# Two transformer blocks with routed experts: a third buffer for routed rows, 28 scatters a sequence, and k's transposes one step sooner

## The chip, the cores and the metric

The kernel runs on one core of a Trainium2 chip. The metric is the device time of one execution in microseconds; three runs of the kernel before are shown, and one further execution was profiled. The core has TensorE (PE, with its weight loads shown as PEld), VectorE (DVE), ScalarE (ACT), GpSimd (POOL) and SyncE (SP). SP issues most DMAs; POOL issues those whose row addresses are computed at run time.

## The reference

Eight sequences of 512 tokens with 256 features go through two blocks. All arithmetic is float32.

```python
x = x + attention0(layernorm(x))   # 16 query heads, 4 key/value heads of 16, rotary, causal
x = x + ffn0(layernorm(x))         # 32 experts, 8 per token, inner 96, weights renormalized over the 8
x = x + attention1(layernorm(x))   # 16 heads of 16, biases, scores masked with -10000
x = x + ffn1(layernorm(x))         # 16 experts, 2 per token, inner 176, and 2 shared experts
```

An expert computes `silu(x @ wg) * (x @ wu) @ wd`, and the token's routing weight scales its result.

## The kernel before

**Stages.** Attention 0 runs over the eight sequences, then all experts of block 0, then attention 1 over the sequences, then all experts of block 1. Tokens are sent to experts through DRAM: each token's normalized row, with its routing weights behind it (288 floats, 1152 bytes), is scattered into the slab of each of its 8 experts (`xg`, L470), one scatter for 128 tokens and one of the 8 choices. A sequence so has 4 x 8 = 32 scatters of 144 KB. The expert stage loads tiles of 128 rows from the slabs (L1339), multiplies them, and writes the results to `yg`.

**Attention 0** is written as a plan for TensorE. Each round treats one sequence in ten steps. A step begins with the scores of some heads (L745), then ScalarE's exp over 2048 columns (L750), then the letters of that step's word in `PLAN0`: "c" a product with the values (L768), "t" the transposes of its result (`ot`, L780, freed by VectorE's product L784), "m" the causal masks (L756), and one step of a chain for "p" and "q" (the next sequences' load, projection, rotary and transposes, `before`, L997), "a" and "o" (the last sequences' output projection, layernorm and routing, `finish`). "q" becomes "p" and "a" becomes "o" in the next round. What is left of a chain at the end of a round is drained there, in the order p, o. The scores have a single PSUM buffer of four banks (`st`), and all small products share three banks in turn (`bank`).

`before` has ten steps: two for loading, one for the statistics, four for the tokens' projections, two for the transposes of q (L1053), and one for k: four transposes (L1059) and two scaled copies on ScalarE (L1062, L1063). For sequence 1 two more steps come first. Three of them run as "q" in one round. In the next round six run as "p", so that k's step is the one that the drain does. At the end of the round in which sequence 3's chain is drained, the tables for the experts' tiles are made as well (`tables`; products `ex` L1238 and `ro` L1240).

**Routed rows.** `layernorm_steps` writes the normalized rows (`xn_f`, L361) to a tile of the pool `xn_rows`, which has two buffers; `route` adds the weights and puts the 32 scatters on the list `waiting`, in step 1 of the round two after that of their sequence. `send` takes scatters off the list: at each step of attention 0 as many as `SENT[0]` says, each paced by (that is, made to wait for) the step's exp. So 32 leave in a round. A buffer is written again only after its scatters have landed. The last sequence is routed in the expert stage.

**The expert stage** of block 0 is a pipeline over pairs of tiles: `load` in step s, the transposes of the rows in step s+4 (L1353), gate and up in s+5 (L1385), the transposes of h in s+6 (L1404), down in s+7 (L1414, copied out by L1419). There are 53 pairs in a first part, which holds only rows of sequences 0 to 3, and 86 in a second, which waits for every scatter. The down weights (`dw`, L1536) are asked for in step 3 of the program; SP issued three of their six DMAs ahead of the first row loads. From step 7 on, two waiting scatters are sent in each step, paced by that step's copy (`beside.made`).

The lines that set the order and its numbers:

```python
PLAN0 = "ocmoo otom poaaom mc taapma comapa tpm qqqm cmpp taaam"
SENT = ((3, 3, 4, 3, 3), (1, 1, 1, 1, 1))      # by step modulo 5; first entry: attention 0
send(SENT[att.n][at % len(STEPS)], None if att.n else att.newest)
if s >= stages[-1][1]:                          # expert stage, step 7 and later
    send(2, beside.made)
```

Of the kernel before, what the change touches and what calls it, by code (L numbers as in the profile page):

```python
# [8 lines left out]
F32 = mybir.dt.float32  # L9
# [8 lines left out]
P = 128  # L18
NB, T, D = 8, 512, 256
NT = T // P  # L20
ND = D // P
H, HKV, DH = 16, 4, 16
NG = 4
# [5 lines left out]
N1 = N1R + IS1  # L29
C0 = N0 // P  # L30
C1 = -(-N1 // P)
PLAN0 = "ocmoo otom poaaom mc taapma comapa tpm qqqm cmpp taaam"
TAIL0 = "otoaoaoaoa"
PLAN1 = "cooggm ootggm oaggm coaggm toapggm acoggpm taaopggm ppaoggm caopggm taopppm"
TAIL1 = "otaaoaaaoaoaoaa"
PB = (3, 2)
SENT = ((3, 3, 4, 3, 3), (1, 1, 1, 1, 1))
SPLIT = (4, 6)
AHEAD = 3
FIRST = 18  # L40
# [60 lines left out]
def two_blocks_kernel(  # L101
# [14 lines left out]
    nc = tc.nc  # L116
# [167 lines left out]
    kept = {}  # L284
# [23 lines left out]
    def inverse_root(var, lnp, name):  # L308

        v = lnp.tile([P, NT], F32, tag="v", name=f"v_{name}")  # L310
        nc.vector.tensor_scalar(v, var, LN_EPS, None, ALU.add)
        bits = lnp.tile([P, NT], I32, tag="bits", name=f"bits_{name}")
        nc.vector.tensor_scalar(bits, v.bitcast(I32), 1, None, ALU.arith_shift_right)
        r = lnp.tile([P, NT], F32, tag="rstd", name=f"rstd_{name}")
        nc.vector.tensor_scalar(r.bitcast(I32), bits, -1.0, float(0x5F3759DF), ALU.mult, ALU.add)
        w = lnp.tile([P, NT], F32, tag="w", name=f"w_{name}")
        for _ in range(3):
            nc.vector.scalar_tensor_tensor(w, r, -0.5, r, ALU.mult, ALU.mult)
            nc.vector.tensor_tensor(w, w, v, ALU.mult)
            nc.vector.scalar_tensor_tensor(r, w, 1.5, r, ALU.add, ALU.mult)  # L320
        return r
# [13 lines left out]
    lasting, turned0, roots, sums = [], [], {}, {}  # L335

    def layernorm_steps(x, lnp, name, tag="xn", bufs=1, spare=0, behind=lambda: None):


        def later():  # L340
            return tc.issue_after(behind()) if behind() else ExitStack()

        stats = lnp.tile([P, NT, 6], F32, tag="stats", name=f"stats_{name}")
        mv = lnp.tile([P, NT, 2], F32, tag="mv", name=f"mv_{name}")
        for t in range(NT):
            with later():
                nc.vector.bn_stats(out=stats[:, t, :], in_=x[:, t, :])
            nc.vector.bn_aggr(out=mv[:, t, :], in_=stats[:, t, :])
            if t % 2:
                yield  # L350
        with later():
            rstd = inverse_root(mv[:, :, 1], lnp, name)
        roots[name] = rstd
        yield
        if tag is None:
            return rstd
        kept = lasting and tag == "xn_rows"
        xn = (lasting[0] if kept else lnp).tile([P, NT, D + spare], F32, tag=tag, name=f"xn_{name}", bufs=2 if kept else bufs)
        for t in range(NT):
            with later():  # L360
                nc.vector.tensor_scalar(  # L361
                    xn[:, t, :D], x[:, t, :], mv[:, t, 0:1], rstd[:, t : t + 1], ALU.subtract, ALU.mult
                )
            if t % 2:
                yield
        return xn
# [484 lines left out]
    def send(n, pace):  # L851
        for work, t, i in waiting[:n]:
            work(t, i, pace)
        del waiting[:n]

    def planned(att, before, after, plan, tail, ahead=None):
# [15 lines left out]
        for b in range(NB):  # L872
# [5 lines left out]
            for at, works in enumerate(plan.split()):  # L878
                att.scores(b, at)
                send(SENT[att.n][at % len(STEPS)], None if att.n else att.newest)  # L880
                drain(begun)
# [32 lines left out]
            )  # L914
        return wo

    def v_tiles(pool, n, heads, engine):

        tiles = []
        for i in range(n):  # L920
            v1 = pool.tile([P, NT, heads * (DH + 1) + 32 - DH - 1], F32, tag="v1", name=f"v1_{i}", bufs=n)
            engine.memset(v1, 1.0)
            tiles.append(v1)
        return tiles
# [4 lines left out]
    def fast0(awp, lnp, atp, late, ptp, ps, bank):  # L929
# [25 lines left out]
        kept = {0: ahead[0]}  # L955
# [6 lines left out]
        turn = []  # L962
        for which in ("cos", "sin"):
            lo, hi = A0[which]
            f = awp.tile([DH, T], F32, tag="turnf", name=f"{which}f", bufs=1)
            nc.scalar.dma_start(out=f, in_=a0[:DH, lo:hi])
            tr = bank(f"{which}t")[:, : NT * DH].rearrange("p (t d) -> p t d", t=NT)
            for t in range(NT):
                nc.tensor.transpose(tr[:, t, :], f[:, t * P : (t + 1) * P], ident[:DH, :DH])
            w = awp.tile([P, NT, DH], F32, tag=which, name=f"{which}0")  # L970
            nc.vector.tensor_copy(w, tr)
            turn.append(w)
        cos, sin = turn
        v1s = v_tiles(awp, 2, NG, nc.gpsimd)
        n_h = H + HKV
        hf = DH // 2

# [322 lines left out]
    def experts(n, gu, dn, mp, ps, again, beside, load_last):  # L1300

        name = f"m{n}{'g' * again}"
# [139 lines left out]
        with tc.manual_schedule(engines={ENG.PE}):  # L1442
            for s in range(len(jobs) + stages[-1][1]):
                for stage, lag in stages:
                    if 0 <= s - lag < len(jobs):
                        stage(*jobs[s - lag])
                if s == 3:
                    load_last()
                beside.step(s)
                if s >= stages[-1][1]:  # L1450
                    send(2, beside.made)
            beside.finish()

    def most_rows(b, again):
# [153 lines left out]
    def drain(part):  # L1608
        for _ in part:
            pass  # L1610
# [119 lines left out]
    with ExitStack() as s2:  # L1730
        lasting.append(s2.enter_context(tc.tile_pool(name="xn_rows", bufs=2, reuse_waits="tile")))
        PARTS = 4
        with ExitStack() as s:
            awp, lnp, atp, late, ptp, smp, ps = pools(s, 0, False)
            bank = banks(ps, 3)
            att, before = fast0(awp, lnp, atp, late, ptp, ps, bank)
            route, _ = ffn_parts(smp, bank)
            gw0 = gpool.tile([P, E0 * GU0], F32, tag="gu", name="gw0")

            def after0(b):  # L1740
                if b == NB - 1:
                    return
                kept = keep_x(b, x_after[0])
                yield from routed0(b, lnp, bank, route)
                if b < PARTS:
                    with tc.issue_after(kept):
                        load_gate_up(gw0, f0, I0, N0, b, PARTS)
                if b == 1:
                    yield from biases1(smp, bank)
                if b == SPLIT[0] - 1:  # L1750
                    yield from tables(lays[0], smp, bank, 0)


            with tc.manual_schedule(engines={ENG.PE}):
                planned(att, before, after0, PLAN0, TAIL0)


        with ExitStack() as s1:
            wp1 = s1.enter_context(tc.tile_pool(name="attn_w1", bufs=1, reuse_waits="tile"))
            gat = s1.enter_context(tc.tile_pool(name="gather", bufs=1, reuse_waits="tile"))  # L1760
            w1, loads1 = weights1(wp1)
            last = all_experts(0, gw0, gat, weights=loads1)
            with ExitStack() as s:
                awp, lnp, atp, late, ptp, smp, ps = pools(s, 1, False)
                v1s = v_tiles(awp, 2, H, nc.vector)
                bank = banks(ps, 3)
                att, before = fast1(w1, v1s, lnp, atp, late, ptp, ps, bank, last)
                route, shared = ffn_parts(smp, bank)
                gw1 = gpool.tile([P, E1 * GU1], F32, tag="gu", name="gw1")

                def ahead1(b):
                    if b >= AHEAD:
                        fetched = fetch_x(b, x_after[0], "a1")
                        with tc.issue_after(fetched):
                            load_gate_up(gw1, f1, I1, N1R, b - AHEAD, NB - AHEAD)
                        yield
                        yield from gathers(b)

                def after1(b):
                    name = f"f1_{b}"  # L1780
                    xn = layernorm(xs[b], lnp, name, "xn_rows", 2, 2 * E1)
                    yield
                    xT = yield from turned(xn, lnp, bank, name)
                    yield from route(1, b, xn, xT, name, False)
                    yield from shared(w1["s"], xT, xs[b], name)
                    if b < NB - RING:
                        keep_x(b, x_after[1])
                    if b == SPLIT[1] - 1:
                        yield from tables(lays[1], smp, bank, 0)

                with tc.manual_schedule(engines={ENG.PE}):
                    planned(att, before, after1, PLAN1, TAIL1, ahead1)
                out_of = not_fine(bank)
        lasting.clear()
# [245 lines left out]
```

## Time and profile before

| | us |
|---|---|
| median of three runs | 1529.74 (1527.24 to 1532.12) |
| the profiled execution | 1526.4 |
| its span, first to last instruction | 1524.7 |
| first exp of attention 0 | 30.25 |
| first expert row loads issued by SP | 378.37 |
| first copy of an expert result (L1419) | 399.0 |
| TensorE busy | 1386.1 (91%) |
| VectorE busy | 949.7 (62%) |
| GpSimd busy | 812.7 (53%) |
| ScalarE busy | 654.7 (43%) |

Of GpSimd's 812.7 us, 326.7 are the 320 scatters of routed rows of both blocks (L470, 1021 ns each, with a gap of 0.30 us after each), and 402.5 are the 256 gathers of the first experts' results (L1494). The table comes from the first part of the page and from the engines' instructions in order of time. Durations in the text are of the one profiled execution. A row of waits reads: who waited, for whom, total us, how many times, the longest.

### The profile page before, as it was taken

The numbers are of one execution on the slowest core, as the hardware profiler recorded it, in microseconds if no ns is written. First come the engines' busy times: TensorE is split into PE (matmuls) and PEld (weight loads), VectorE is DVE, ScalarE is ACT, GpSimd is POOL, SyncE is SP. The second block draws the span as 40 slices with busy tenths as digits, with TensorE's granted clock in tenths as the row PEclk, the third lists the DMA queues.
The fourth block names the chain that finished last, engine by engine and source line by source line (L and its number), as shares of the span: only waits on it lengthen the run. The fifth ranks groups of instructions, "written<-read, shape, count | busy, mean of one in ns | idle before, by whom it ended". The sixth has DMA issues, their size and how long they took to land.

```text
span 1524.7 us, 29311 instructions
## 1 busy us (share of the span) xinstructions
PE 1386.1 (91%) x9608; PEld 951.1 (62%) x9608; DVE 949.7 (62%) x3141; ACT 654.7 (43%) x857; POOL 812.7 (53%) x674
## 2 busy tenths in 40 slices
PE   5788988887899999999997889999999988999994
PEld 3444544444789889999894445455465454777773
DVE  4668888876475557655565567677577564544454
ACT  2556666654233323333334546646646642122222
POOL 0004777777366100288878887788887204243342
PEclk8999999999899999999999999999999999999996
DMA  2023555435999786899998555665553015353346
GB/s 82 15 70 99 162 166 164 151 135 155 296 298 294 251 254 197 225 259 269 269 271 163 70 70 104 101 146 84 114 70 91 32 31 177 96 173 111 117 159 232
DMA packets 229311, 237.20 MB, mean 156 GB/s; under 512 B 77820, under 2 KB 209281, under 8 KB 229154
## 3 DMA queue, kind: packets, MB, share of 16 engines
q1 hardware_dynamic: 172930, 145.73, 32.4%
q0 software_dynamic: 55872, 89.18, 25.4%
q8 instruction: 83, 1.36, 0.4%
q14 instruction: 74, 0.61, 0.1%
q10 hardware_dynamic: 352, 0.33, 0.1%
HBM read 125.79 MB, written 110.92 MB: 155 GB/s over the span
## 4 chain that ended last, share of the span: by engine, by line
PE 58%; POOL 11%; issue 5%; DMA 4%; DVE 3%; ACT 3%; SPq 0%; DVEq 0%; ACTq 0%; POOLq 0%
PE gu_m L1385 18%; PE y_m L1414 12%; POOL x_a L1494 10%; PE xgT_m L1353 5%; PE st_a L745 4%; PE o_a L768 3%; PE hT_m L1404 3%; ACT p_a L750 2%; PE sg_f L503 2%; PE sy_f L516 2%; PE su_f L503 2%; PE y_a L842 1%; PE v_a L1129 1%; DMA xg<-xn_f,rows_f 1%; DMA xg_m<-xg 1%
## 5 line engine op out<-in xcount | busy, mean ns | idle before, releaser
L1494 POOL DMA_INDIRECT x_a<-yg,yrows x256 | 402.5, 1572 | 218.0 <-DMA xg_m<-xg 131.0
L470 POOL DMA_INDIRECT xg<-xn_f,rows_f x320 | 326.7, 1021 | 344.0 <-ACT sums L1023 131.1
L750 ACT ACTIVATE p_a<-st_a 128x2048 f32<-128x2048 f32 x160 | 300.4, 1877 | 187.0 <-PE st_a L745 85.3
L1385 PE MATMUL gu_m<-gw,xgTs_m 128*128 x1416 | 304.4, 359 | 1.2 <-DVE xgTs_m L1355 1.2
L1385 PEld LDWEIGHTS gu_m<-gw,xgTs_m 128*128 128x128 f32 x1416 | 236.3, 193 | 26.0 <-DVE xgTs_m L1355 1.7
L745 PE MATMUL st_a<-qT_a,kT_a 32*128 32x512 f32 (+3 forms) x2048 | 192.7, 480 | 58.8 <-ACT p_a L750 49.2
L1414 PE MATMUL y_m<-dw,hTs_m 96*128 (+1 forms) x860 | 215.8, 380 | 2.1 <-issue 2.1
L756 DVE TENSOR_TENSOR p_a<-p_a,causal 128x512 f32<-128x512 f32 x256 | 169.6, 687 | 74.1 <-ACT p_a L750 73.7
L1419 ACT COPY ys_m<-y_m 128x512 f32<-128x512 f32 x177 | 103.6, 585 | 170.0 <-PE y_m L1414 150.9
L745 PEld LDWEIGHTS st_a<-qT_a,kT_a 32*128 32x128 f32 x2048 | 92.2, 190 | 133.5 <-ACT p_a L750 72.8
L1355 DVE COPY xgTs_m<-xgT_m 128x512 f32<-128x512 f32 x177 | 121.5, 687 | 80.0 <-PE xgT_m L1353 75.7
L768 PE MATMUL o_a<-p_a,v 128*32 128x512 f32 (+3 forms) x2048 | 158.9, 450 | 3.6 <-DVE p_a L756 3.6
L1414 PEld LDWEIGHTS y_m<-dw,hTs_m 96*128 96x128 f32 (+1 forms) x860 | 149.7, 190 | 16.1 <-issue 2.3
L1377 DVE SCALAR_TENSOR_TENSOR h_m<-h_m,xg_m,gu_m 128x96 f32<-128x96 f32 (+1 forms) x354 | 104.2, 325 | 83.1 <-ACT h_m L1390 39.1
L1427 POOL DMA_INDIRECT yg<-ys_m,to_m x76 | 80.3, 1057 | 125.8 <-ACT ys_m L1419 113.1
L768 PEld LDWEIGHTS o_a<-p_a,v 128*32 128x32 f32 x2048 | 57.7, 112 | 122.0 <-issue 92.0
L1405 DVE COPY hTs_m<-hT_m 96x256 f32<-96x256 f32 (+1 forms) x177 | 84.0, 474 | 76.0 <-PE hT_m L1404 75.6
L1393 ACT ACTIVATE h_m<-gu_m 128x192 f32<-128x192 f32 x139 | 45.9, 330 | 181.2 <-PE gu_m L1385 162.1
L1353 PE MATMUL xgT_m<-ident,xg_m 128*128 128x128 f32 x708 | 110.3, 278 | 11.2 <-DMA xg_m<-xg 7.3
L1353 PEld LDWEIGHTS xgT_m<-ident,xg_m 128*128 128x128 f32 x708 | 88.4, 143 | 33.3 <-issue 9.4
L1404 PE MATMUL hT_m<-ident,h_m 128*96 128x128 f32 (+1 forms) x430 | 76.8, 274 | 0.0
L1404 PEld LDWEIGHTS hT_m<-ident,h_m 128*96 128x96 f32 (+1 forms) x430 | 52.8, 125 | 16.7 <-issue 6.4
(266 smaller groups left out, 1591.7 us busy)
## 6 DMA issues: line engine op xcount, KB each, us to landing
xg_m<-xg SPq DMA_DIRECT2D x354, 144.0 KB
yg<-ys_m SPq DMA_DIRECT2D x139, 256.0 KB
g<-yg SPq DMA_DIRECT2D x16, 512.0 KB
xg<-zeros SPq DMA_DIRECT2D x50, 144.0 KB
xg<-xn_f,rows_f POOLq DMA_INDIRECT x320
x_after<-x_in SPq DMA_DIRECT2D x8, 512.0 KB
x_a<-x_after SPq DMA_DIRECT2D x8, 512.0 KB
x_a<-yg,yrows POOLq DMA_INDIRECT x256
```

Source lines behind the costliest of these rows:

```text
L470: inst = nc.gpsimd.indirect_dma_start(out=lay.xg, out_offset=bass.IndirectOffsetOnAxis(ap=rows[:, t, i : i + 1], axis=0), in_=xn[:, t, :], ...
L745: nc.tensor.matmul(st[:, g, lo : lo + T - j * P], kT[r, j * P : (j + 1) * P], qT[r, j * P :], start=True, stop=True,)
L750: self.newest = nc.scalar.activation(pt, st, AF.Exp, scale=SCALE).ins
L756: self.masked = nc.vector.tensor_tensor(d, d, causal.unsqueeze(1).to_broadcast([P, NG, P]), ALU.mult).ins
L768: nc.tensor.matmul(o[32 * g : 32 * g + 32, j * P :], v1[:, j, v_at + g * (DH + 1) :][:, :32], pt[:, g, lo : lo + T - j * P], start=(step = ...
L1353: nc.tensor.transpose(tr[:, j, c, :], xg[:, j, c * P : (c + 1) * P], ident)
L1355: nc.vector.tensor_copy(xT, tr)
L1377: nc.vector.scalar_tensor_tensor(h[:, j, :], h[:, j, :], xg[:, j, D:][:, bass.ds(offs[part, i + j][2], 1)], gus[j][:, inner:], ALU.mult, A ...
L1385: nc.tensor.matmul(gus[j], xT[:, j, c, :], gu[:, bass.ds(at + c * 2 * inner, 2 * inner)], start=(c == 0), stop=(c == ND - 1),)
L1404: nc.tensor.transpose(hp[:n_in, q, j, :], h[:, j, lo : lo + n_in], ident)
L1414: nc.tensor.matmul(y[:, j, :], hT[:n_in, q, j, :], dn[:n_in, bass.ds(at + q * D, D)], start=(q == 0), stop=(q == n_ch - 1),)
L1494: inst = nc.gpsimd.indirect_dma_start(out=xs[b][:, t, :], out_offset=None, in_=lay.yg[: most_rows(b, again), :], in_offset=bass.IndirectOf ...
```

## The change

Five edits are made, and nothing of the arithmetic changes.

- `layernorm_steps` gives the rows of sequences 2 and 5 of block 0 a buffer of their own (tag `more_rows`), beside the two that the others share, so that a buffer comes round after three sequences instead of two.
- `SENT[0]` goes from 3, 3, 4, 3, 3 to 3, 3, 2, 3, 3: 28 scatters in a round of ten steps instead of 32.
- In the expert stage, steps 2 to 6 send two scatters each as well, paced by the step's row load (`beside.load`).
- `PLAN0` has a third "p" in step 8. For sequences 2 to 7 that is k's step of `before`; for sequence 1 it is the second of the four projections.
- Two changes of memory: in attention 1 the second tile of values is put into the `more_rows` buffer, and in the start of attention 0 the cos and sin tables are read through the buffer `kr` instead of one of their own.

```diff
-PLAN0 = "ocmoo otom poaaom mc taapma comapa tpm qqqm cmpp taaam"
+PLAN0 = "ocmoo otom poaaom mc taapma comapa tpm qqqm cmppp taaam"
-SENT = ((3, 3, 4, 3, 3), (1, 1, 1, 1, 1))
+SENT = ((3, 3, 2, 3, 3), (1, 1, 1, 1, 1))
...
-        xn = (lasting[0] if kept else lnp).tile([P, NT, D + spare], F32, tag=tag, name=f"xn_{name}", bufs=2 if kept else bufs)
+        if kept and name.startswith("f0_") and int(name[3:]) % 3 == 2:
+            tag, bufs = "more_rows", 1
+        elif kept:
+            bufs = 2
+        xn = (lasting[0] if kept else lnp).tile([P, NT, D + spare], F32, tag=tag, name=f"xn_{name}", bufs=bufs)
...
-    def v_tiles(pool, n, heads, engine):
+    def v_tiles(pools, heads, engine):
...
-        for i in range(n):
-            v1 = pool.tile([P, NT, heads * (DH + 1) + 32 - DH - 1], F32, tag="v1", name=f"v1_{i}", bufs=n)
+        for i, pool in enumerate(pools):
+            tag = "more_rows" if pool in lasting else "v1"
+            v1 = pool.tile([P, NT, heads * (DH + 1) + 32 - DH - 1], F32, tag=tag, name=f"v1_{i}", bufs=pools.count(pool))
...
-            f = awp.tile([DH, T], F32, tag="turnf", name=f"{which}f", bufs=1)
+            f = atp.tile([DH, T], F32, tag="kr", name=f"{which}f", bufs=1)
...
-        v1s = v_tiles(awp, 2, NG, nc.gpsimd)
+        v1s = v_tiles([awp, awp], NG, nc.gpsimd)
...
                 if s >= stages[-1][1]:
                     send(2, beside.made)
+                elif s > 1:
+                    send(2, beside.load)
...
-                v1s = v_tiles(awp, 2, H, nc.vector)
+                v1s = v_tiles([awp, lasting[0]], H, nc.vector)
```

## The prediction

> **What bounds the kernel now.** I read the page's slices first, then a table of windows cut at each sequence of the first attention, then the waits, then single engines in order of time. The change touches three places: the first attention (78 to 376 us of the span), the start of the first expert stage (376 to 404), and the tail of that stage's scatters (to 503). All work is serial across these stages, so a microsecond won or lost on TensorE's path in any of them is one in the total.
>
> The windows, cut at the first exp of each sequence (columns: length; busy time and instructions of PE, PEld, DVE, ACT, POOL; clock; DMA share; GB/s):
>
> ```profile
> 121.60:163.50 41.90, 36.29 (x344) 19.75 (x344) 34.48 (x135) 26.05 (x28) 24.04 (x23) 1.00 0.46 139
> ...
> 206.00:248.00 42.00, 36.12 (x344) 19.71 (x340) 34.44 (x135) 26.00 (x27) 32.24 (x33) 1.00 0.56 175
> 248.00:292.40 44.40, 38.62 (x354) 20.43 (x354) 37.65 (x156) 26.01 (x27) 34.65 (x33) 0.97 0.42 146
> 292.40:334.30 41.90, 37.13 (x336) 19.30 (x336) 30.33 (x115) 25.15 (x25) 32.76 (x31) 0.95 0.38 132
> ```
>
> A sequence takes 42 us whether POOL is busy 24 or 33 us in it; only that from 248 is 2.3 us longer. So the scatters, back to back on POOL from 150 to 384 us, hardly slow the attention. What they could slow is VectorE's write of normalized rows (L361), which waits for a buffer whose scatters have landed, and the waits say what that is worth in all:
>
> ```profile
>   DMA xg<-xn_f,rows_f: 0.7, 3
> ```
>
> Three waits, 0.24 us each. TensorE's own waits over the sequences are these:
>
> ```profile
> PE st_a L745 <- ACT kT_a L1062: 9.5, 7, 1.6
> ...
> PE ro L1240 <- DVE otok_a L784: 1.9, 1, 1.9
> ```
>
> **Third buffer: -0.5 us.** At most the 0.7 us above goes, and only where VectorE leads: the chain of waits runs through it after two of the three (272.7 and 356.5), 2 x 0.24 = 0.5. Rows of sequence s join the waiting list in step 1 of round s+2 and leave from step 2 on. Before, 26 go in that round and 6 in the next two steps, so none is left over. With 28 a round, sequences 0 to 3 finish at round 3 step 3, round 4 step 4, round 5 step 6 and round 6 step 7. The row that reuses their buffer is written about step 5 of rounds 4, 5, 6 and 7, eight steps later at least. No new wait. Without the third buffer, 28 would make one. The shared cos/sin buffer costs nothing: its readers come before the first key write, in TensorE's order already. Nor does attention 1's value tile in the third buffer: sequence 5's scatters, its last readers, land in the expert stage long before.
>
> **k's transposes, five ordinary boundaries: +0.6 us.** This is one boundary now, ScalarE then TensorE:
>
> ```profile
> 200.67 1.07 ACT L1054 COPY qT_a<-qT_a 128x512 f32<-128x512 f32 x2
> 202.21 1.88 ACT L750 ACTIVATE p_a<-st_a 128x2048 f32<-128x2048 f32 x1 [0.47 <-PE st_a L745]
> 203.98 0.68 ACT L1062 ACTIVATE kT_a<-kT_a,half 128x512 f32<-128x512 f32 x1
> 204.55 0.69 ACT L1063 ACTIVATE kT_a<-kT_a,half 128x512 f32<-128x512 f32 x1
> ```
>
> ```profile
> 201.00 1.15 PE L745 MATMUL st_a<-qT_a,kT_a 32*128 32x384 f32 x16
> 202.07 0.66 PE L780 MATMUL ot_a<-ident,osb_a 128*128 128x128 f32 x4
> 202.57 0.60 PE L1059 MATMUL kT_a<-ident,kr_a 128*128 128x128 f32 x4
> 204.72 1.14 PE L745 MATMUL st_a<-qT_a,kT_a 32*128 32x512 f32 x8 [1.55 <-ACT kT_a L1062]
> ```
>
> The wait of 1.55 us looks like the prize, but most of it stays: the scores buffer (one copy) is free only when the exp begun at 202.21 ends. Where nothing but an exp stands ahead, scores start 1.94 us after its start (209.29 to 211.23 in the next steps); here 2.51 (202.21 to 204.72). So the move, which issues no DMA, saves 0.57. It is paid for at once: the four transposes now stand before the 201.00 scores, which follow the q transposes without a gap, +0.55 on TensorE (0.60 less the overlap of the record). ScalarE must also make its two k copies (1.25 us together) after the q copies end at 201.74, so its exp comes near 202.9 instead of 202.21: +0.69. Net 0.12 a boundary. Ends: -0.5 if the exp is not delayed, +0.55 if ScalarE takes it before the k copies (then the wait stays and TensorE's 0.55 is added). I take 0.12, nearest to the order in which the inputs come ready: 5 x 0.12 = 0.6.
>
> **The sequence from 248 us: -2.0 us.** There the end of a round also drains the planner's tables. Products take one of three PSUM banks in turn. Before, the order is q, q, ot, k, ex, ro, so ro gets ot's bank, and ot is freed by a VectorE product that comes late (L784, 289.7): TensorE stands 1.9 us and the next scores follow at 290.23. With k ahead the order is q, q, k, ot, ex, ro: ro gets k's bank, freed by ScalarE some 2 us earlier. The round should fall from 44.4 to the 42 of its neighbours. I take 2.0 of 2.3, since VectorE's masks of the last step end at 291.8 and limit the product after the scores; ends 0 (another VectorE item holds TensorE) and -2.3. **A rule against a row** here: the Trainium skill, "TensorE: Matmul & The Clock Gate", "What's actually happening", has the clock halve after an idle window of about 3.4 us. By it a pause of 1.9 us costs 1.9. The trace shows half clock (0.50) at 290 to 292 after this pause, and the eight scores take 2.02 us against 1.14, some 0.9 more; by the row up to 2.8 would go, capped by the round's own 2.3.
>
> In round 0 (b = 1 has two more steps) the third "p" brings one token's projection forward, not k. VectorE works there almost without a break from 64.5 to 73.8 us and leads; its one gap of 0.3 us fills: **-0.3**.
>
> **Fewer scatters beside attention, more at the experts' start: +0.5 us.** Seven sequences of 32 make 224. Before, 186 leave in the attention and 38 are left; with 28 a round, 162 leave and 62 are left. Ten go in expert steps 2 to 6, two per step, each pair waiting for that step's row load (behind a waiting scatter POOL's queue holds only scatters until the gathers of 634 us); 52 go from step 7, so with sequence 7 the list ends in step 48 instead of 43. The first tile of the second part needs them in step 53. Those five steps are 14 us, to 517 us; that load goes out at 534. Expert steps are 2.82 us with scatters (460 to 480) and without (600 to 650), so this costs nothing; if DMA were full there, up to +3.
>
> The start itself is limited by DMA:
>
> ```profile
> 334.30:386.00 51.70, 37.27 (x364) 19.85 (x356) 29.63 (x116) 24.03 (x20) 37.89 (x39) 0.93 0.52 168
> 386.00:400.00 14.00, 11.27 (x51) 9.83 (x52) 4.95 (x12) 2.86 (x5) 0.11 (x1) 0.74 1.05 264
> ```
>
> ```profile
> 382.80 0.96 POOL L470 DMA_INDIRECT xg<-xn_f,rows_f  x1 [0.30 <-issue]
> 399.89 0.95 POOL L470 DMA_INDIRECT xg<-xn_f,rows_f  x1 [16.13 <-ACT ys_m L1419]
> ```
>
> In the second fence a lagging POOL still scatters at 382.8, then stands 16 us. TensorE begins at 386.05 when the first rows land, and its first down product waits until 397.84, I read for the second half of the down weights (the row says only "issue", but the row loads of 388 to 399 wait 7.1 us for these same weights). What goes: POOL, no longer behind, ends near 376, so about five of the seven scatters after 375 are gone: 5 x 147 KB at 325 GB/s (mean of 378 to 386) = 2.3 us. What comes: the scatters of steps 2 and 3, 4 x 147 KB at 231 GB/s (mean of 388 to 396) = 2.5 us; those of steps 4 to 6 wait for loads issued after the weights. Net +0.2, and a slightly longer pause before that product, +0.3. **The second rule** speaks against the change: "DMA: Bandwidth & Descriptors", "Queues, rings and completion order", says each DMA engine takes queues in turn, packet by packet, so POOL's scatters push into the weights' time however early those were issued. By it all ten could come first: 10 x 147 KB / 231 = 6.4 us less 2.3 = +4.1; by the rows only four can. I take +0.5; ends -4 (rows land 2.3 earlier and the 0.5 clock of 386 to 392 is avoided, with the product not held) and +6.
>
> **Sum:** -0.5 + 0.6 - 2.0 - 0.3 + 0.5 = -1.7 us. Made against the profiled execution, 1526.4 us (span 1524.7) goes to 1524.7. The shown runs have a median 3.3 us above it, 1529.74, so I forecast 1528.0.
>
> **Rivals.** (1) *The ramp opens.* If TensorE's first down product waits for rows, not weights, the five missing scatters and the avoided half clock bring 4 us more, and a k move on the good side (5 x -0.5 instead of +0.6) another 3: 1521. For it: 3.8 us of TensorE idle before 386 and clock 0.5 after. Against: the pause at 396. (2) *The scatters collide with the weights* (slower): steps 2 to 6 put ten scatters before the last weights, +4 to +6 at the ramp, and the bank gain is lost to VectorE: 1529.74 - 0.2 + 5 = 1534.5. It decides once more than some eight scatters land before the down weights. (3) *The k move and the third buffer both cancel*: 1529.7, if ro merely waits for something else.
>
> **Chances.** The derived case 0.50 (1525 to 1529.5), rival 1 0.20, rival 2 0.20, rival 3 0.10. About 0.3%, 4.6 us, is what a measurement here tells from no change. Faster: rival 1 and a fifth of the derived case, 0.30; slower: rival 2 and a little of 3, 0.22; the rest 0.48. Range 1519 to 1535, from the far side of rival 1 to that of rival 2.
>
> **What would show it.** POOL with gaps in each round and done near 376; L361's waits gone; TensorE's wait for kT gone but exps 0.5 to 0.7 us later in step 9; round 5 near 42 us; ten scatters between 385 and 402; the first down product within 2 us of its old place after attention ends. If rounds 2 to 4 differ by more than 0.5 us, or the first down product moves by more, the sum is wrong.

## The result: 0.63% slower

The changed kernel takes 1538.11 us (median of six runs, 1535.47 to 1540.83) where the kernel before takes 1528.22 (six runs, 1526.3 to 1532.12): a ratio of 1.0063 [1.0051, 1.0076]. On another chip, later, it was 1542.23 against 1527.02, 1.0099 [1.0082, 1.0116]. The forecast was 1528.0, the range ended at 1535.

**Where the time went.** ScalarE's exps (160, one for each step of the attentions) and its copies of expert results (177) mark the stages. This table has the lengths between such marks in one profiled execution of each kernel, all on chips where an ordinary round takes 42 us. "p alone" and the others are experiments of the next section.

| us | before | changed | changed, sw1 first | p alone | sends alone |
|---|---|---|---|---|---|
| attention 0, first to last exp | 340.6 | 339.0 | 337.9 | 338.0 | 343.3 |
| of it, the round from 248 us | 44.4 | 42.5 | 42.5 | 42.5 | 44.5 |
| to the first copy of expert stage 0 | 28.2 | 29.2 | 28.6 | 30.7 | 36.5 |
| expert stage 0, first to last copy | 404.9 | 407.2 | 406.6 | 401.8 | 410.1 |
| attention 1, first to last exp | 433.5 | 434.1 | 433.1 | 433.7 | 434.9 |
| to the first copy of expert stage 1 | 65.8 | 73.8 | 66.9 | 66.1 | 67.2 |
| expert stage 1, first to last copy | 182.0 | 184.2 | 182.0 | 182.0 | 182.0 |

The changed kernel's last copy is 13.5 us later than before's: 10.2 of them arise at the start of the second expert stage, some 900 us after the last step of the plan that was changed. The first attention is 1.6 us shorter and pays for the rest only in part.

**The start of the second expert stage, after.** Its down weights `dw` are 26 loads on SP's queue (the edits moved the line numbers: L1536 of before is L1543 in the changed kernel). First the kernel before, then the changed one, in order of time (columns: start, length, queue, line, what, count):

```profile
1250.82 13.61 SPq L1536 DMA_DIRECT2D dw<-in_f_dram  x26
1265.96 8.63 SPq L1339 DMA_DIRECT2D xg_m<-xg  x14
```

```profile
1254.16 6.51 SPq L1344 DMA_DIRECT2D xg_m<-xg  x11
1302.27 13.02 SPq L1543 DMA_DIRECT2D dw<-in_f_dram  x26
1315.51 5.88 SPq L1344 DMA_DIRECT2D xg_m<-xg  x9
```

Before, the weights were issued 59 us ahead of the first product that uses them (1310.11), beside attention 1's last work. After, they go out at 1302.27. The row of SP's waits says for what:

```profile
SPq L1543 <- PE sy_f L520: 41.5, 1, 41.5
```

`sy_f` is the last product of the shared experts, the end of attention 1. Of TensorE in order of time:

```profile
1296.59 5.60 PE L520 MATMUL sy_f<-sw,hs_f 128*128 128x256 f32 x24
...
1313.15 0.60 PE L1409 MATMUL hT_m<-ident,h_m 128*88 128x128 f32 x4
1319.52 3.75 PE L1419 MATMUL y_m<-dw,hTs_m 88*128 x8 [5.78 <-DMA xg_m<-xg]
...
1324.36 4.27 PE L1390 MATMUL gu_m<-gw,xgTs_m 128*128 x8
```

TensorE finishes `sy_f`, does what needs no down weights, and stands from 1313.7 to 1319.5. The row names a row load as the one that came last by the profile, but the product's other operand is `dw`, whose 26 loads are issued from 1302.3 to 1315.3. Before, this product stood at 1310.11, straight after the transposes, and its eight took 1.89 us. Here they take 3.75, and the next gate and up products 4.27 instead of 2.53. The windows show why (columns: length; busy time and instructions of PE, PEld, DVE, ACT, POOL; clock; DMA share; GB/s):

```profile
1302.00:1313.00 11.00, 10.19 (x51) 6.97 (x51) 6.24 (x18) 1.58 (x5) 0.00 (x0) 1.00 0.66 174
1313.00:1318.00 5.00, 0.75 (x6) 0.34 (x3) 0.99 (x2) 0.32 (x1) 0.00 (x0) 0.96 0.87 205
1318.00:1325.00 7.00, 5.48 (x16) 4.05 (x17) 1.93 (x12) 0.58 (x1) 0.78 (x1) 0.50 0.92 280
```

After the pause the granted clock is 0.50 for the next 7 us, half of what it was before, and the eight products take twice as long. Measured from the last exp, the first copy is 8.0 us later than before, the second 10.25, and all others up to the last 10.25: one pause and the half clock after it, nothing else.

**Why SP waits for `sy_f`.** Tiles are allocated in pools, and pools are stacked in each partition's memory. `xn_rows`, at the bottom of this stack, lasts from attention 0 to attention 1; above it stands the pool of attention 1's weights, with `sw1`, the shared experts' weights, last. When all these are closed, `dw` of stage 1 is laid at a place that does not depend on them. The addresses in the two programs (bytes in a partition):

```
           sw1 (read by sg_f, su_f, sy_f)   dw, stage 1
before     129120 .. 138336                 141920 .. 174688
changed    133728 .. 142944                 141920 .. 174688
```

The third buffer adds 4,608 bytes to `xn_rows`, all above it moves up, and the last 1,024 bytes of `sw1` come to lie under the first 1,024 of `dw` (142944 - 141920). This is called the overlay below. Before, 3,584 bytes lay between them. A load may not overwrite what is still to be read, so it waits for `sy_f`, the last reader of `sw1`.

**Attention 0, after.** The windows that answer to those of before, cut at the first exps of the same sequences:

```profile
205.70:247.90 42.20, 36.27 (x344) 19.74 (x341) 34.63 (x136) 25.91 (x27) 29.14 (x29) 1.00 0.52 161
247.90:290.40 42.50, 37.43 (x354) 20.24 (x350) 36.06 (x154) 25.92 (x27) 29.39 (x29) 1.00 0.39 136
290.40:331.80 41.40, 36.63 (x336) 19.16 (x332) 31.48 (x119) 25.05 (x25) 31.48 (x29) 0.96 0.36 127
```

The second row was 44.40 us. At its end TensorE now does this:

```profile
287.12 0.66 PE L784 MATMUL ot_a<-ident,osb_a 128*128 128x128 f32 x4
287.71 0.34 PE L1243 MATMUL ex<-past,step 32*1 32x106 f32 x2
287.89 0.34 PE L1245 MATMUL ro<-past,nt 32*1 32x106 f32 x2
289.33 1.14 PE L749 MATMUL st_a<-qT_a,kT_a 32*128 32x512 f32 x8 [1.11 <-ACT p_a L754]
```

`ro` follows `ex` without a gap, at full clock, where it had stood 1.9 us for VectorE's `otok`. An ordinary boundary, ScalarE then TensorE:

```profile
200.63 1.07 ACT L1059 COPY qT_a<-qT_a 128x512 f32<-128x512 f32 x2
201.59 0.70 ACT L1067 ACTIVATE kT_a<-kT_a,half 128x512 f32<-128x512 f32 x1
202.17 0.70 ACT L1068 ACTIVATE kT_a<-kT_a,half 128x512 f32<-128x512 f32 x1
202.74 1.90 ACT L754 ACTIVATE p_a<-st_a 128x2048 f32<-128x2048 f32 x1
```

```profile
200.87 0.60 PE L1064 MATMUL kT_a<-ident,kr_a 128*128 128x128 f32 x4
201.40 1.15 PE L749 MATMUL st_a<-qT_a,kT_a 32*128 32x384 f32 x16
...
204.69 1.14 PE L749 MATMUL st_a<-qT_a,kT_a 32*128 32x512 f32 x8 [1.55 <-ACT p_a L754]
```

TensorE's wait is as long as before, 1.55 us, under another name: for the exp, no longer for kT. In the four rounds from 78 to 248 us the tenth exp follows the ninth 0.55 to 0.6 us later than before, and the next round's first exp gives 0.55 back.

**The scatters, after.** GpSimd at the end of attention 0, and SP's first row loads:

```profile
370.14 0.96 POOL L474 DMA_INDIRECT xg<-xn_f,rows_f  x1 [0.30 <-issue]
371.41 0.96 POOL L474 DMA_INDIRECT xg<-xn_f,rows_f  x1 [0.30 <-issue]
...
382.81 0.96 POOL L474 DMA_INDIRECT xg<-xn_f,rows_f  x1 [0.30 <-issue]
400.19 0.95 POOL L474 DMA_INDIRECT xg<-xn_f,rows_f  x1 [16.43 <-ACT ys_m L1424]
```

```profile
377.73 7.95 SPq L1344 DMA_DIRECT2D xg_m<-xg  x8
```

From 371.41 to 382.81 run the ten scatters of expert steps 2 to 6. None waited for its step's load: the first five stand before the first load at all, and in the program's list of instructions these ten wait for ScalarE or for earlier scatters only. A likely reason, not tried by itself, is that the load is a member of a group ("full0") and the scatter is declared free of dependences on that group, which takes this one along.

### The profile page after: what moved, and what is told of

Same layout as the page of the kernel before. It is cut to its first block, busy times and chain, and to the rows that moved or that the text cites. A ratio compares the mean times of both kernels' runs of the same rounds, so it can differ in the third digit from the quotient of the medians.

```text
span 1536.7 us, 29328 instructions
## 1 busy us (share of the span) xinstructions
PE 1392.0 (91%) x9608; PEld 954.7 (62%) x9608; DVE 949.5 (62%) x3141; ACT 653.7 (43%) x857; POOL 813.0 (53%) x674
## 4 chain that ended last, share of the span: by engine, by line
PE 59%; DVE 7%; POOL 6%; DMA 4%; issue 3%; ACT 3%; SPq 1%; DVEq 0%; ACTq 0%; POOLq 0%
PE gu_m L1390 16%; PE y_m L1419 11%; PE st_a L749 5%; PE xgT_m L1358 5%; POOL x_a L1501 5%; PE o_a L772 4%; PE hT_m L1409 3%; ACT p_a L754 2%; PE sg_f L507 2%; PE su_f L507 2%; PE v_a L1134 2%; PE sy_f L520 1%; PE q_a L1148 1%; PE k_a L1153 1%; DMA xg<-xn_f,rows_f 1%
## 5 line engine op out<-in xcount | busy, mean ns | idle before, releaser
L474 POOL DMA_INDIRECT xg<-xn_f,rows_f x320 | 327.6, 1024 | 365.9 <-ACT sums L1028 138.4
L1410 DVE COPY hTs_m<-hT_m 96x256 f32<-96x256 f32 (+1 forms) x177 | 84.0, 474 | 73.8 <-PE hT_m L1409 73.5
```

The source lines that it names most:

```text
L474: inst = nc.gpsimd.indirect_dma_start(out=lay.xg, out_offset=bass.IndirectOffsetOnAxis(ap=rows[:, t, i : i + 1], axis=0), in_=xn[:, t, :], ...
```

## The experiments

There are eight edits and the changed kernel once more, in sixteen runs. The first eight runs fell on two chips where the kernel before takes 1661.82 and 1646.06 us instead of 1526.6 to 1528.7; the last section shows what differs there. Totals of those chips are compared only with each other, and for the main questions the same kernels were run again elsewhere.

**1. `sw1` first in its pool.** The changed kernel, one allocation moved; under the first KB of `dw` then lies the value bias, whose last reader is early.

```diff
     def load(out, in_):
         loads.append((out, in_))
+    w["s"] = sw1 = pool.tile([P, NS, 2 * ND * P + D], F32, tag="sw1", name="sw1")
...
-    w["s"] = sw1 = pool.tile([P, NS, 2 * ND * P + D], F32, tag="sw1", name="sw1")
     for n in range(NS):
```

> The changed kernel, with one tile placed elsewhere: the shared experts' weights sw1 stand first in the second attention's weight pool instead of last, so that the last KB of that pool, which the last stage's down weights overlie, is the value bias and not sw1. Theory 1 (overlay): the down weights' loads of the second expert stage are issued by 1257 us instead of 1302, its first down product comes 8 to 11 us sooner than in the changed kernel, and the time falls from 1538.1 to 1527 to 1530. Theory 2 (scatters and the longer tail in the first block set the loss, the late weights are hidden): within 1.5 us of the changed kernel, 1536.5 to 1539.5.

> The changed kernel with sw1 first in its pool, again, because the first four runs fell on a chip where the attention's rounds took some 55 us instead of 42 and hid small differences. There the last exp of the second attention and the second expert stage's first down product lay 65.8 us apart with this edit, as in the kernel before (65.8), and 74 us with the overlay. Theory 1 (overlay): 1527.5 to 1530 where the kernel before takes 1528: all of the loss but 0 to 2 us is gone. Theory 2 (the first block's 3.3 us remain and grow): 1531 to 1535.

> The changed kernel with sw1 first, on the same chip as the changed kernel. Theory 1 (overlay): 8 to 11 us faster than it, with 65.5 to 67 us between the last exp and that product; beside the kernel before, within 1.5 us where the attention's rounds take 42 us, and faster by 10 us or more where they take 50 to 60 (there fewer scatters a round are worth more). Theory 2: within 2 us of the changed kernel.

On the first two chips it took 0.9918 [0.9886, 0.995] and 0.99 [0.9865, 0.9935] of the kernel before (there the four scatters fewer a round outweigh the rest, see experiment 4), with 65.8 and 67.0 us between the last exp and the first copy of stage 1. On the third, 1529.07 us against 1527.02: 1.0012 [0.9997, 1.0026], and 13.2 us under the changed kernel on the same chip. SP's queue in that run:

```profile
1250.26 6.44 SPq L1345 DMA_DIRECT2D xg_m<-xg  x11
1256.88 13.57 SPq L1544 DMA_DIRECT2D dw<-in_f_dram  x26
```

The weights are 45 us earlier, the wait for `sy_f` is gone, and the second stage takes 182.0 us again. The order on the queue (rows, then weights) stayed that of the changed kernel. It is not told from costing nothing: the stretch to the first copy is 66.9 us here and 65.8 on the first chip, while kernels with the old order have 65.8 to 67.2. Most of the loss is the overlay.

**The changed kernel beside it:**

> The changed kernel once more, beside its version with sw1 first on the same chip. Theory 1 (overlay): 8 to 11 us slower than that version, whatever the chip's attention takes; the last exp of the second attention and the first down product of the second expert stage lie 73.5 to 74.5 us apart. Theory 2 (the loss is in the first block): within 2 us of that version.

1542.23 us, 13.2 over the version with `sw1` first; 75.3 us between exp and copy. The gap is larger than I expected. In the two profiles the stretches that hold it differ by 8.4 (to the first copy) and 2.6 us (the stage), and attention 1 by 1.6.

**2. The third buffer alone.** From the changed kernel, the sends of before and no third "p":

```diff
-SENT = ((3, 3, 2, 3, 3), (1, 1, 1, 1, 1))
+SENT = ((3, 3, 4, 3, 3), (1, 1, 1, 1, 1))
-PLAN0 = "ocmoo otom poaaom mc taapma comapa tpm qqqm cmppp taaam"
+PLAN0 = "ocmoo otom poaaom mc taapma comapa tpm qqqm cmpp taaam"
-                elif s > 1:
-                    send(2, beside.load)
```

> The third buffer alone: sends (32 a sequence, none in expert steps 2 to 6) and k's transposes as before; the third row buffer, the value tile in it and the shared cos/sin buffer as in the change. Theory 1 (overlay): the down weights of the second expert stage are again issued near 1300 us, and the time is 8 to 11 us over the kernel before, 1536 to 1539, with the first block within 1 us of before. Theory 2 (scatters): within 1 us of the kernel before.

On the first chip 1670.25 us against 1661.82: 1.0054 [1.0031, 1.0077], 8.4 us. The last exp and the first copy lie 74.1 us apart (65.8 with `sw1` first there), the stage takes 183.8, and the down weights go out at 1433.98, 52 us after the last exp. So the buffer brings the late weights and the loss of this stretch with neither sends nor plan. The total is weaker evidence than these lengths, since the attention varies more on that chip.

**3. The third "p" alone**, one letter in the kernel before.

> The kernel before with the third p in the plan and nothing else. Theory 1: the round from 248 us is 2.3 to 2.5 us shorter, the other rounds as before at their ends, and the second expert stage starts its down products as before: 1525.5 to 1526.5, 2 us under before. Theory 2 (a gain in the first attention is given back at the last round or at the experts' start): within 0.7 us of before.

> The kernel before with the third p alone, again on another chip. Theory 1: the round from 248 us is 2.3 to 2.5 us shorter and 2 us under before is left at the end. Theory 2: the last round, whose pause for VectorE and ScalarE ends at half clock, gives 1.6 us back: within 1 us of before.

> The kernel before with the third p alone. Where the kernel before takes about 1527 us, Theory 1: the round from 248 us is 2.3 to 2.5 us shorter, nothing else moves by more than 1 us up to the second attention, 2 us under before. Theory 2: the last round gives 1.6 us back at half clock, within 0.7 us of before. Where the attention's rounds take over 50 us, the run tells nothing about the third p.

> The kernel before with the third p alone, in more rounds, to see whether the 2.2 us that its trace shows from the round at 248 us on are in the time as well. Theory 1: 0.9985 of the kernel before, with 1 outside the interval. Theory 2 (the start of the experts takes it back, since GpSimd's last scatters end as late as before): 0.999 to 1.0005. Where the attention's rounds take over 50 us, it tells nothing of this.

On the first two chips 1.0061 [1.0042, 1.0081] and 1.0032 [1.0003, 1.0061], slower than the kernel before there; why is not known, and rounds of 50 to 63 us hide the 2 us in question. On two others 1525.47 against 1527.71, 0.9993 [0.998, 1.0007], and 1526.69 against 1526.63, 0.9994 [0.9983, 1.0004]. The round from 248 us is 42.5 us, as in the changed kernel. But the time from the last exp to the first copy grows from 28.2 to 30.7: GpSimd is behind and starts its last scatter of the attention at the same time (383.5 against 382.8), so the experts' start does not follow the attention. In the second of these the last round also took 38.3 us (36.5 before), so that the attention as a whole gained only 0.5. By the two intervals the gain is at most 3 us and not told from none: no version that is faster than the kernel before beyond doubt.

**4. The sends alone**, on the kernel before with its two buffers.

```diff
-SENT = ((3, 3, 4, 3, 3), (1, 1, 1, 1, 1))
+SENT = ((3, 3, 2, 3, 3), (1, 1, 1, 1, 1))
                 if s >= stages[-1][1]:
                     send(2, beside.made)
+                elif s > 1:
+                    send(2, beside.load)
```

> The kernel before with the sends of the change (28 a sequence, two in each of expert steps 2 to 6) and nothing else: two row buffers, old plan, old memory. Theory 1: the list of scatters ends some 14 to 22 us later, the row loads of the second part wait 2 to 3 us more for it at step 53, and the time is 1530 to 1531.5; the ten scatters of steps 2 to 6 run before the first row load, with no wait for one. Theory 2 (the tail is hidden): within 0.7 us of before. With two buffers VectorE's normalized rows may wait for late scatters in the first attention; by my prediction they do, up to 2 us in a round.

> The kernel before with the change's sends alone, again on another chip. Theory 1: the list of scatters ends 22 us later, the wait for the second part's rows near step 53 grows by 2 to 3 us, and the start of the experts does not move: 1.5 to 3 us over before. Theory 2 (hidden): within 0.7 us of before.

> The kernel before with the change's sends alone. Where the kernel before takes about 1527 us, Theory 1: the list of scatters ends 22 us later and the first expert stage, from its first down product to its last, is 1.7 to 2.3 us longer, as in the changed kernel; the rounds do not change: 1.5 to 3 us over before. Theory 2: within 0.7 us of before. Where the attention's rounds take over 50 us, fewer scatters a round save 10 us or more and the total says nothing of the tail.

On the first two chips 0.9872 [0.9793, 0.9951] and 0.9891 [0.985, 0.9932]; four scatters fewer a round are worth 18 to 29 us there. On the third, 1545.57 us against 1527.71: 1.0118 [1.0102, 1.0134], both theories off by far. VectorE's wait for its buffer of rows, feared in the last sentence of the first expectation, is the main reason, in a place and of a size that were not expected:

```profile
391.79 1.38 DVE L361 TENSOR_SCALAR xn_f<-x_in,mv_f,rstd_f 128x256 f32<-128x256 f32 x4 [14.14 <-DMA xg<-xn_f,rows_f]
```

The last sequence's normalized rows need the buffer whose scatters are still on the list, now longer. VectorE stands 14.1 us, behind it everything that the start of the experts needs of VectorE, and the first copy comes 11.9 us later than before: 8.3 of them after the last exp, 2.8 in the attention, where one more such wait takes 2.5 us. Without the third buffer these sends lose more than they could win.

**5. Third buffer and third "p", old sends, `sw1` first.**

> The changed kernel with sw1 first and the sends of before (32 a sequence, none in expert steps 2 to 6): third buffer and third p are kept. Theory 1 (the changed sends cost 3 to 4 us in the first expert stage, which the round from 248 us pays for): first expert stage as long as in the kernel before (404.5 to 405.5 us from first to last down product instead of 406.6), 1.5 to 2.5 us under the kernel before in all. Theory 2 (the third buffer itself costs, by the memory it moves): the same as with the changed sends, 0 to 2 us over before.

1528.28 us against 1528.66: 0.9996 [0.9985, 1.0008]. With the changed sends it was 1.0012 [0.9997, 1.0026]; the intervals overlap, so the sends' cost is not told from nothing, and is hardly over 5 us. Its first expert stage took 406.4 us with the old sends, against 406.6 with the new: the first expectation, that the changed sends make this stage 2 us longer, fell with that.

The part that the third buffer itself costs is seen when the start is added to the stage, from the last exp of attention 0 to the last copy of expert stage 0. Without the third buffer this takes 432.5 to 433.2 us (before and "p alone", three profiles). With it, it takes 435.2 to 436.6 us (four profiles), with the old sends as with the new, so some 2 to 4 us belong to the buffer. A part of them can be named. Attention 1's second value tile now lies in that buffer, and VectorE fills it (L927) in the middle of the expert stage, when it needs the buffer free. The changed kernel:

```profile
433.50 1.01 DVE L927 MEMSET v<- 128x1148 f32 x1 [0.57 <-DMA xg<-xn_f,rows_f]
```

It waits for sequence 5's scatters, 0.57 us here, 1.5 when the changed kernel ran again. In this experiment VectorE stands 3.8 us before it (the row there names a row load as the last to come), and the sixth copy follows the fifth after 4.9 us instead of 2.8. The rest of the 2 to 4 us was not traced.

**6. No scatters in expert steps 2 to 6** (the changed kernel, `sw1` first, without the two lines `elif s > 1: send(2, beside.load)`), and the same with 30 scatters a sequence:

> The changed kernel with sw1 first and no scatters in expert steps 2 to 6; from step 7 two a step as before, so the list ends ten scatters later. Theory 1 (the ten run beside the first row loads and hold the ramp; DMA sets it): the last exp of the first attention and the first down product lie 25.5 to 27.5 us apart instead of 28.6 to 29.6, and the wait near step 53 grows by 3 to 5 us: 1527 to 1532. Theory 2 (the weights set the ramp): ramp unchanged, time 3 to 5 us over the version with them.

> As the run before, with 30 scatters a sequence instead of 28, so that some twelve scatters fewer are left for the expert steps. Theory 1: the ramp is short by the same 2 to 3 us, the list ends where the changed kernel's does, and with the round from 248 us the time is 1523 to 1526, under both kernels. Theory 2: ramp unchanged, 1526 to 1529.

1538.46 and 1534.85 us against 1528.66: 1.006 [1.0038, 1.0082] and 1.0041 [1.0023, 1.0058]. The profile of the first is of its fastest execution (1532.62). GpSimd in it:

```profile
374.48 0.96 POOL L474 DMA_INDIRECT xg<-xn_f,rows_f  x1 [0.30 <-issue]
396.78 0.96 POOL L474 DMA_INDIRECT xg<-xn_f,rows_f  x1 [21.34 <-ACT ys_m L1425]
```

Here GpSimd is done at 375.4, and the start opens: 26.4 us from exp to first copy, against 28.6 to 29.6 with the ten. So scatters beside the first row loads do hold the start, by some 2 to 3 us in these profiles. The price is higher: with 62 scatters left, TensorE's waits for row loads near step 53 are 9.4 us in all (4.6 with the ten, 3.5 before), and the stage takes 413.9 us; the median missed the expected 1527 to 1532. With thirty a sequence the start is 27.8 and the stage 412.1. That version was expected under both kernels, and missed by 10 us. Of this, 7.9 us lie between the tenth and the eleventh copy of the stage, 10.7 us apart instead of 2.8. VectorE and TensorE there:

```profile
428.81 1.01 DVE L927 MEMSET v<- 128x1148 f32 x1 [6.90 <-DMA xg<-xn_f,rows_f]
```

```profile
430.43 2.93 PE L1391 MATMUL gu_m<-gw,xgTs_m 128*128 x8 [6.17 <-DVE xgTs_m L1361]
```

It is the value tile in the third buffer once more: VectorE stands for sequence 5's scatters, which leave later in this version, its copies stand behind it, and TensorE waits for them. In the version with 28 a sequence the same instruction waits 4.2 us. Another 3.4 us of the thirty version lie at the start of the second expert stage (69.3 us from the last exp to the first copy) and were not traced. So neither version shows what the opened start alone is worth.

**7. Three scatters a step from step 7**, and none in steps 2 to 6:

> The changed kernel with sw1 first, no scatters in expert steps 2 to 6, and three instead of two a step from step 7. Theory 1: ten scatters fewer run before the first row loads (the ramp is 1 to 3 us shorter) and the list ends near step 38, so the wait at step 53 is at most that of before: 1522 to 1526. Theory 2: with three a step DMA is full, each of some 30 steps is longer by 0.1 us or more, and the time is 1528 to 1532.

On the second chip 1651.09 us, 1.0025 [1.001, 1.004], where edit 1, with two a step and the ten in steps 2 to 6, took 0.99 of the kernel before. The 45th copy follows the first after 184 us, with two a step after 150. Three scatters take 3 x 1.26 us on GpSimd, more than a step's 2.8 us; why TensorE follows GpSimd there was not settled, nor was it run on a chip with 42 us rounds.

## Why the prediction was wrong

**The step that failed** is the one sentence on memory in the step of the third buffer: "Nor does attention 1's value tile in the third buffer: sequence 5's scatters, its last readers, land in the expert stage long before." The buffer's place in memory stands at nothing there. The sentence asked who uses the new buffer, not what the buffer moves. Its growth put `sw1` under `dw` and made a load that had been issued 59 us ahead of its use wait for the end of attention 1: 10.2 us in the profile, 8 to 13 by the runs. None of the rivals had it; the diff showed the buffer, and the old profile the load, issued 51 us earlier than now, but the addresses were not worked out. The reason that the sentence gives is wrong too: the tile is filled in the middle of the expert stage (433.5 us), and sequence 5's scatters have not landed "long before", since VectorE waits for them, 0.57 us in the changed kernel and 6.9 with thirty a sequence (experiment 6).

Without the overlay the changed kernel lies at 1.0012 [0.9997, 1.0026], where 0.9989 had been forecast (1528.0 to 1529.74). So the overlay is not all of the error: the forecast gain is excluded without it as well. The attention did gain (2.7 us in that profile, 2.2 forecast), and the start and first expert stage together gave 2.1 back, where 0.5 had been forecast.

**Third buffer, -0.5.** VectorE's wait for its rows stayed in part: 0.5 us in two waits instead of 0.7 in three. The statement that without the third buffer 28 scatters would make a wait was right (experiment 4); the largest one, at the last sequence, was 14 us.

**k's transposes, +0.6.** The forecast had the exp 0.69 us later and 0.57 saved behind it. Measured are 0.55 to 0.6 later and 0.55 given back, and in place of TensorE's wait for k stands as long a wait for the exp. So the mechanism was right, and the size is 0.0 a boundary instead of 0.12.

**The round from 248 us, -2.0.** Right in place and cause. Between first exps it is 1.9 us in the changed kernel's profile, and 2.4 between second exps (44.9 to 42.5 us), where the half clock after the pause is in the length as well: from 290 to 292 us the granted clock was 0.50 before and is 1.00 now. The forecast by the pause alone (1.9) and the one with the half clock (up to 2.8) thus enclose it. What was not foreseen is the last round: 38.1 us instead of 36.5, and 37.7 and 38.3 with the third p alone. So the whole attention gained 0.5 to 2.9 us in the eight profiles with that letter on chips with 42 us rounds.

**Round 0, -0.3.** Not to be seen: 47.1 to 48.0 us in kernels with the third p, 47.8 without.

**Scatters and the start, +0.5.** The sum came near, +0.9, +0.3 and +1.4 us in three profiles, by another way, so this is luck. "GpSimd ends near 376" and "each pair waiting for that step's row load" are both wrong: the ten were not held, ran straight on from the attention's last ones, and the last of them began at 382.8 as before. So five scatters were not gained, and none was issued beside the second half of the weights (386.4), where four had been counted. Experiment 6 shows the predicted end (375.4) and an opened start where there are no ten. Rival 2 is answered in the same way: all ten did land ahead of the last weights, which it took for 4 to 6 us, but they stood in the place of as many of the attention's own late scatters, so that this stretch was as full before.

**Five more steps of the list, 0.** The count was off: before, the list ends behind the 35th copy, in step 41 and not 43, so it is seven steps, and the last scatter begins at 525.3 instead of 502.4 us, 22.8 later and not 14. That this costs nothing is neither shown nor refuted: the stage was 1.7 to 2.3 us longer in three profiles with these sends, but 1.5 longer in one without (experiment 5). A list longer still, to 553.4 us, did cost (experiment 6), so the row of steps "with scatters and without" was the wrong witness: the wait at step 53 decides, not the length of a step.

## What to carry to other kernels

A buffer's price is also what it moves and what is put into it. When a pool that lasts grows, list which tiles change their neighbours, above all which later load then lies over a tile that is read late; here one allocation's place was worth 13 us. Ask of each new tenant of a buffer when its first write comes, not only when its last reader was meant to be done. A dependence that is meant as a pace holds only if the trace shows the wait. And a gain ahead of a stage whose start hangs on another engine (here GpSimd's last scatters) can be lost there.

## What was not expected of the hardware

The same program ran at two speeds on different chips. "p alone", the same round (from its 41st exp to its 51st), first on the chip where it took 1525.47 us, then on the one where it took 1654.89:

```profile
205.80:247.90 42.10, 36.19 (x344) 19.74 (x340) 34.62 (x135) 25.91 (x27) 32.34 (x33) 1.00 0.56 176
```

```profile
230.80:291.60 60.80, 44.02 (x344) 22.66 (x340) 34.75 (x134) 25.77 (x28) 32.75 (x33) 0.86 0.39 122
```

VectorE, ScalarE and GpSimd are busy as long, for as many instructions. TensorE is busy 44.0 us instead of 36.2, of which the lower clock explains most (36.2 / 0.86 = 42.1). All of them wait more. The second expert stage, from its first copy to its last, takes 182.0 us on both chips. The long stretches are those with GpSimd's indirect DMAs beside other work: in the kernels with 32 scatters a sequence the rounds with scatters take 51 to 63 us, the first two rounds, which have none, 42 to 48 as elsewhere. The length of a scatter and the gap between two (0.96 and 0.30 us) are the same. That the scatters are the cause is likely, since four fewer a round saved 18 to 29 us there, but what holds the engines stays open.
